# Seven products instead of eight for the first batch's Z, with the factors summed by accumulating transfers

## The chip, the cores and the metric

The kernel runs on one core of a Trainium2 chip. The metric is device time in microseconds for one execution. The kernel before was run three times: median 541.52 us (541.51 to 541.65). One execution more was profiled; the durations below are from that one.

## The reference

Four batches of 1024 tokens with 512 channels pass through one block of attention and a linear layer, each modulated by channels that come from a small conditioning vector:

```
mod = (silu(c) @ wmod), six vectors per batch: sa, ca, ga, sb, cb, gb
ga, gb = sign * max(|.|, 0.25)
h = layernorm(x) * (1 + ca) + sa
A = softmax over j of (h Wq^T)(h Wk^T)^T      (the same scores for all 16 heads)
x = x + ga * ((A (h Wv^T)) Wo^T)
h = layernorm(x) * (1 + cb) + sb
x = x + gb * (h @ (sum of 8 factors) / sqrt(8) + bias)
```

All is float32. The eight factors are 512 x 512 each; since their outputs are added, the kernel adds the factors first and multiplies once.

## The kernel before, in words

All heads have the same attention matrix, so per batch the kernel forms Z = N^T P^T, where N is the normalised input (1024 x 512) and P the exponentials of the scores (1024 x 1024, not yet divided by their sums). The output is then Z times one 512 x 512 matrix w (`make_w`, L696), which holds Wv, Wo, 1 + ca and ga. The reciprocal sums are multiplied in as a tile of output is added to x (L725); the shift sa becomes a row c1 that is added to every token (`add_c1`, L408).

Work is in tiles of 128 tokens, eight to a batch, in two groups ("halves") of four. Per batch, in the order in which the program is written:

- `ln1` (L395): statistics on VectorE, a power on POOL (L351), normalisation on VectorE (L365). Then the transposed copy: by TensorE for batch 0 (L378), for later batches by 32 x 32 transposes on VectorE (L437) and 16 DMAs that move blocks (`move_blocks`, L416 to L426, on SP's queue unless others are given).
- `scale_wqk` (L450): four multiplications on VectorE of the projection's weights by 1 + ca. `project` (L458): queries and keys of one half.
- `scores` (L505) for a pair of tiles: eight matmul records, a maximum on VectorE (L531), exponentials on ScalarE (L535). `transpose_probs` (L540) turns them by VectorE (L544) and 16 block moves; the first two pairs of batch 0 go through TensorE (`transpose_probs_pe`, L550), copied from PSUM by ScalarE (L561).
- Z in two halves of 512 columns. Batch 0 uses `z_steps` (L572): for each of four row blocks eight accumulated matmuls of 128 x 128 by 512 columns, and a copy by ScalarE (L592). In the trace each float32 matmul is two records, 128 in all. Batches 1 to 3 use `z_steps_by_seven` (L636): N and P are cut into quarters, and Z's four quarters come from seven products of sums of quarters (Strassen's method in the form with 15 additions). The sums of N are on POOL (`n_sums`, L612, lines L620 to L623, once a batch), those of P on VectorE (`p_sums`, L630, L633 and L634; L662 and L667 during the products), the sums of products on VectorE from PSUM (L672, L674, L677, L682, L688), two on POOL (L678, L679) and two copies on ScalarE (L660, L665). Each product is 16 records with 256 columns.
- `attn_out` (L716): four matmuls per tile of output, an addition to x on VectorE, statistics for the second layernorm.
- `ln2` (L734): as ln1, transposed by VectorE and block moves, scaled on ScalarE (L765). `make_f` (L705) multiplies the factor sum by gb on VectorE (L713); `ffn` (L771) is the last product, and its result goes out by DMA. `ffn` of one batch runs among the products of the next batch's Z.

What sets the order: each engine has its own queue, worked in order, and waits for semaphores in it. The steps have priorities that follow the text of the program, and a planner orders each engine's queue when the kernel is built, by its own estimate of when inputs are ready; `tc.keep_in_program_order` pins an instruction behind whatever was written before it on its engine. DMAs are issued from SP, ScalarE (ACT) and POOL; a DMA whose inputs are not ready holds up that engine's queue.

The parts around the change:

- The main loop for b = 0 (L821 to L841): Z's first half, the last softmax pair, `ln1` and the transposed copy of batch 1, `shift_rows` (c1 from its PSUM rows), `gates` (the two gates with `publish`, which stores rows to DRAM, L308), the eight c1 additions (L837), `second_channels`, `sum_factors`.
- `sum_factors` (L325): 16 loads of 512 KB on POOL's queue into four staging tiles of the pool `stg`, and 28 additions on POOL (L337, L340). A copy of one element by ScalarE (L331) keeps the first four from starting before Z's third row block is done.
- `spread` (L239) loads one row from DRAM to all 128 partitions, into two tiles with the tag "bc".
- Z's second half (L865 on): between its steps come batch 1's two projections and three softmax pairs (`places`), `make_w` after step 1; behind it `n_sums` of the next batch and `attn_out`, `ln2`, `p_sums` of the next batch.
- PSUM: four buffers of 512 columns (`psum_mm`) and two of 1024 for scores.

Of the kernel before, what the change touches and what calls it, by code (L numbers as in the profile page):

```python
# [30 lines left out]
def kernel(  # L31
# [19 lines left out]
    P = 128  # L51
# [273 lines left out]
    def sum_factors():  # L325
        for kc in range(KC):
            for r in range(0, NR, 2):
                f = stage(f"factor_{kc}_{r}").rearrange("p (r d) -> p r d", r=2)
                if kc == 0:

                    nc.scalar.copy(f[0:1, 0, 0:1], ZT[0, 0][0:1, 2, 0:1])  # L331
                nc.gpsimd.dma_start(
                    out=f, in_=factors[r : r + 2, ts(kc, P), :].rearrange("r p d -> p r d")
                )
                acc = fsum[:, kc, :]
                if r == 0:
                    nc.gpsimd.tensor_tensor(acc, f[:, 0], f[:, 1], ALU.add)  # L337
                else:
                    for k in range(2):
                        nc.gpsimd.tensor_tensor(acc, acc, f[:, k], ALU.add)  # L340
# [65 lines left out]
    bc_c1 = {}  # L406
# [21 lines left out]
    def hT_by_dma(b, g):  # L428
# [9 lines left out]
        move_blocks(st, hT.rearrange("p r k w -> p r (k w)"))  # L438
        return hT
# [100 lines left out]
    def transpose_probs(b, p):  # L540

        half, pair = divmod(p, 2)
        pr2 = probs[b, p][0]
        nc.vector.transpose(pr2, pr2)  # L544
        move_blocks(
            pr2.rearrange("p (c n) -> p c n", c=NQ),
            pt_tile(b, half)[:, pair].rearrange("p r j w -> p r (j w)"),
        )
# [17 lines left out]
    def softmax(b, p):  # L566
        scores(b, p)
        transpose_probs(b, p)

    ZT = {}  # L570

    def z_steps(b, half):  # L572

        zt = ztp.tile([P, KC, GW], F32, tag="zt", name=f"zt_{b}_{half}")
        ZT[b, half] = zt
        hold, steps = {}, []

        def part(dc, jh):
            if jh == 0:
                hold[dc] = psum_mm(f"ps_z_{b}_{half}_{dc}")  # L580
            for j in halves(jh):
                nc.tensor.matmul(  # L582
                    hold[dc], xn1[b, jh][:, j - jh * GT, ts(dc, P)], PT[b, half][:, :, :, j, :],
                    start=(j == 0), stop=(j == NT - 1),
                )
            if jh == 1:
                dst, src = zt[:, dc, :], hold[dc]
                if by_dma(b, half):

                    dst = dst.rearrange("p (h t r a) -> p h r t a", h=2, t=2, r=NQ)  # L590
                    src = src.rearrange("p (h r t a) -> p h r t a", h=2, t=2, r=NQ)
                nc.scalar.copy(dst, src)  # L592

        for dc in range(KC):
            for jh in range(2):
                steps.append(lambda dc=dc, jh=jh: part(dc, jh))
        return steps
# [38 lines left out]
    def z_steps_by_seven(b, half):  # L636
# [8 lines left out]
        def product(k, a, m):  # L645
            ps = psum_mm(f"ps_z_{b}_{half}_m{k}")
            for dc in range(2):
                for j in range(GT):

                    nc.tensor.matmul(  # L650
                        ps[:, ts(dc, 2 * P)], a[:, j, ts(dc, P)],
                        m[:, :, j].rearrange("p r (k a) -> p k r a", k=2),
                        start=(j == 0), stop=(j == GT - 1),
                    )
            return ps.rearrange("p (d i) -> p d i", d=2)
# [40 lines left out]
    def make_w(b):  # L696
        bc = spread("ga", b)
# [102 lines left out]
    for step in hT0[1][1]:  # L800
        step()
    first_channels(part)
# [10 lines left out]
    for jp in range(NT // 2):  # L813
        transpose_probs_pe(0, 1, jp)
    mod_rows(ps_mod_b, 4, rows_b)
# [3 lines left out]
    for b in range(B):  # L819
        nb = b + 1 if b + 1 < B else None  # L820
        if b == 0:  # L821
            z0 = z_steps(b, 0)
            z0[0]()
            softmax(0, 3)
            ln1(1, 0)
            hTn = [hT_by_dma(1, 0)]
            shift_rows(ps_c1)
            for step in z0[1:3]:
                step()
            ln1(1, 1)  # L830
            hTn.append(hT_by_dma(1, 1))
            gates()
            scale_wqk(nb)
            for step in z0[3:5]:
                step()

            add_c1(0, range(NT))  # L837
            for step in z0[5:]:
                step()
            second_channels()  # L840
            sum_factors()  # L841
        else:
            z0 = z_steps_by_seven(b, 0)
# [29 lines left out]
        for k, step in enumerate(z1):  # L873
# [3 lines left out]
            if b > 0 and k >= 3 and (nb is not None or k < 5):  # L877
# [62 lines left out]
```

## Time and profile before

| what | number |
|---|---|
| median of three runs | 541.52 us |
| the profiled execution, its own time | 538.85 us |
| its span, first to last instruction | 537.0 us |
| first record of Z, batch 0 | 56.84 us |
| first product of batch 1 (seven products) | 161.29 us |
| first product of batch 2 | 281.16 us |
| mean granted clock of TensorE | 0.996 |
| factor loads, first issue to last POOL addition | 80.95 to 145.6 us |

How to read it: the page has the busy time of each engine, the span in 40 slices, groups of equal instructions with mean durations, the chain of work that ended last, and DMA issues with the time to landing. The trace also answers for any stretch of the span. PE is TensorE, PEld its weight loads, DVE VectorE, ACT ScalarE, POOL GpSimd, SP the sync engine. Records of matmuls overlap: the sum of their durations is more than the time from the first to the last.

### The profile page before, as it was taken

Reading aid. Unit: us, or ns where it says so; the run is one execution under the profiler, and the core shown is the slowest. Engines: PE = TensorE matmul, PEld = TensorE weight load, DVE = VectorE, ACT = ScalarE, POOL = GpSimd, SP = SyncE. Lnnn points to the kernel's source line nnn. Section 1 sums busy time; section 2 is a strip of 40 time slices with the busy share of each in tenths; the row PEclk is TensorE's granted clock in tenths of the full one; section 3 lists DMA queues with packets and bytes.
Section 4 is the critical chain, followed back from the end, with each engine's and each line's share of the span. In section 5 each row is a group of like instructions: output and inputs, shape, how many; then the busy total and the mean of one; then the engine's idle time right before and its main releaser. Section 6 shows DMA issues by size and latency. Waiting matters only on the chain.

```text
span 537.0 us, 5254 instructions
## 1 busy us (share of the span) xinstructions
PE 523.4 (97%) x1688; PEld 290.9 (54%) x1688; DVE 362.1 (67%) x580; ACT 93.2 (17%) x155; POOL 158.5 (30%) x177
## 2 busy tenths in 40 slices
PE   6999899999999999999999999999999999999997
PEld 3533344433448457766448457765448457855444
DVE  4629987264899974359999965358999315577761
ACT  1327500122302020123102010123202200000110
POOL 1002136999801353323001343323001134021010
PEclk9989999999999999999999999999999999999999
DMA  8942369858444667404444656404444415001142
GB/s 319 380 182 68 89 179 262 247 165 244 109 118 113 174 209 226 134 1 97 118 113 113 183 157 209 110 0 99 122 119 107 142 59 214 21 0 32 47 157 78
DMA packets 39570, 74.07 MB, mean 138 GB/s; under 512 B 9988, under 2 KB 10756, under 8 KB 39544
## 3 DMA queue, kind: packets, MB, share of 16 engines
q1 hardware_dynamic: 27368, 41.06, 26.8%
q0 software_dynamic: 8624, 28.48, 17.0%
q10 hardware_dynamic: 3552, 4.21, 2.9%
q8 instruction: 13, 0.21, 0.2%
q14 instruction: 13, 0.11, 0.1%
HBM read 35.93 MB, written 8.42 MB: 83 GB/s over the span
## 4 chain that ended last, share of the span: by engine, by line
PE 58%; DVE 20%; issue 8%; SPq 5%; DMA 4%; POOL 3%; ACT 2%; DVEq 0%; POOLq 0%; ACTq 0%
PE ps_z_m L650 17%; PE ps_f L779 15%; PE ps_z L582 8%; PE ps_qk L469 5%; PE ps_o L720 5%; SPq L426 5%; PE ps_wvo L186 3%; DVE pr L544 3%; DVE nm L531 2%; DMA pt<-pr 2%; PE ps_sc L515 2%; ACT pr L535 2%; DVE hT_f L365 2%; DVE x L725 1%; DVE bn_a L356 1%
## 5 line engine op out<-in xcount | busy, mean ns | idle before, releaser
L779 PE MATMUL ps_f<-f,hT_f 128*128 128x512 f32 (+1 forms) x264 | 111.8, 580 | 0.8 <-ACT hT_f L765 0.5
L720 PE MATMUL ps_o<-w,zt 128*128 128x512 f32 x256 | 111.8, 594 | 0.5 <-DVE zt L688 0.5
L779 PEld LDWEIGHTS ps_f<-f,hT_f 128*128 128x128 f32 x264 | 49.9, 190 | 59.4 <-issue 54.3
L720 PEld LDWEIGHTS ps_o<-w,zt 128*128 128x128 f32 x256 | 48.3, 190 | 61.2 <-issue 56.4
L650 PE MATMUL ps_z_m<-pt,xn_a 128*128 128x256 f32 x288 | 65.3, 380 | 0.0
L650 PEld LDWEIGHTS ps_z_m<-pt,xn_a 128*128 128x128 f32 x288 | 54.6, 190 | 11.4 <-issue 2.4
L582 PE MATMUL ps_z<-pt,xn_a 128*128 128x512 f32 x128 | 56.9, 597 | 0.0
L784 DVE TENSOR_TENSOR x<-ps_f,x 128x512 f32<-128x512 f32 (+1 forms) x33 | 21.9, 670 | 43.8 <-PE ps_f L779 43.8
L535 ACT ACTIVATE pr<-ps_sc,nm 128x1024 f32<-128x1024 f32 x32 | 35.5, 1111 | 79.1 <-DVE nm L531 40.9
L650 PE MATMUL ps_z_m<-pt,s 128*128 128x256 f32 x192 | 43.6, 380 | 0.0
L650 PEld LDWEIGHTS ps_z_m<-pt,s 128*128 128x128 f32 x192 | 36.3, 190 | 8.5 <-issue 3.9
L582 PEld LDWEIGHTS ps_z<-pt,xn_a 128*128 128x128 f32 x128 | 23.8, 190 | 31.6 <-issue 30.8
L515 PE MATMUL ps_sc<-kT,qT 64*128 64x512 f32 x128 | 38.2, 626 | 2.3 <-ACT pr L535 2.3
L531 DVE TENSOR_REDUCE nm<-ps_sc 128x1 f32<-128x1024 f32 x32 | 37.6, 1210 | 2.4 <-PE ps_sc L515 2.4
L765 ACT ACTIVATE hT_f<-st_f,mod_sb,mod_cb 128x512 f32<-128x512 f32 x28 | 20.6, 803 | 96.6 <-DVE bn_f L356 40.2
L351 POOL TENSOR_TENSOR r_f<-v_f,mhalf 128x4 f32<-128x4 f32 x8 | 9.3, 1165 | 94.8 <-DVE v_f L347 94.8
L725 DVE SCALAR_TENSOR_TENSOR x<-ps_o,ri,x 128x512 f32<-128x512 f32 x32 | 23.8, 743 | 15.1 <-PE ps_o L720 15.0
L544 DVE STREAM_TRANSPOSE pr<-pr 128x2048 f32<-128x2048 f32 x14 | 32.2, 2299 | 0.9 <-DMA pt<-pr 0.7
L351 POOL TENSOR_TENSOR r_a<-v_a,mhalf 128x4 f32<-128x4 f32 x8 | 9.2, 1152 | 78.8 <-DVE v_a L347 78.6
L340 POOL TENSOR_TENSOR fsum<-fsum,factor 128x512 f32<-128x512 f32 x24 | 30.4, 1273 | 0.4
L469 PE MATMUL ps_qk<-hT_a,wqk 128*128 128x512 f32 x64 | 30.5, 624 | 0.0
L483 DVE TENSOR_SCALAR qT<-ps_qk,qbias 64x512 f32<-64x512 f32 x8 | 5.9, 743 | 36.1 <-PE ps_qk L469 36.1
(124 smaller groups left out, 582.7 us busy)
## 6 DMA issues: line engine op xcount, KB each, us to landing
pt<-pr SPq DMA_DIRECT2D x224, 64.0 KB, 2.0
factor<-in_factors_dram POOLq DMA_DIRECT2D x16, 512.0 KB, 5.1
hT_a<-st_a SPq DMA_DIRECT2D x96, 64.0 KB, 4.9
out_dram<-x POOLq DMA_DIRECT2D x24, 256.0 KB, 2.6
x<-in_x_dram POOLq DMA_DIRECT2D x24, 256.0 KB, 5.3
xa<-in_x_dram POOLq DMA_DIRECT2D x20, 256.0 KB, 4.0
st_f<-hT_f SPq DMA_DIRECT2D x62, 64.0 KB, 2.0
st_f<-hT_f ACTq DMA_DIRECT2D x60, 64.0 KB, 2.1
```

Source lines behind the costliest of these rows:

```text
L340: nc.gpsimd.tensor_tensor(acc, acc, f[:, k], ALU.add)
L426: queues[i % len(queues)].dma_start(out=dst[ts(c, Q), r], in_=src[ts(r, Q), c])
L469: nc.tensor.matmul(ps[: 2 * R, :], wqkb[b][:, kc, :], hT[:, kc] if b == 0 else hT[:, :, kc], start=(kc == 0), stop=(kc == KC - 1),)
L515: nc.tensor.matmul(ps[:, ts(h, 512)], qT[h * R : (h + 1) * R, ts(i, P)], kT[h * R : (h + 1) * R, :], start=True, stop=True,)
L531: nc.vector.tensor_reduce(nm, ps, AX.X, ALU.max, negate=True)
L535: nc.scalar.activation(pr, ps, AF.Exp, bias=nm, scale=1.0, accum_out=den[:, k : k + 1])
L544: nc.vector.transpose(pr2, pr2)
L582: nc.tensor.matmul(hold[dc], xn1[b, jh][:, j - jh * GT, ts(dc, P)], PT[b, half][:, :, :, j, :], start=(j == 0), stop=(j == NT - 1),)
L650: nc.tensor.matmul(ps[:, ts(dc, 2 * P)], a[:, j, ts(dc, P)], m[:, :, j].rearrange("p r (k a) -> p k r a", k=2), start=(j == 0), stop=(j == ...
L720: nc.tensor.matmul(ps, ZT[b, half][:, kc, ts(j, P)], wb[b][:, kc, :], start=(kc == 0), stop=(kc == KC - 1),)
L725: nc.vector.scalar_tensor_tensor(xi, ps, rinv[b][:, t : t + 1], xi, ALU.mult, ALU.add)
L779: nc.tensor.matmul(ps, hT2[b, g][:, kc, ts(j, P)], fb[b][:, kc, cols], start=(kc == 0), stop=(kc == KC - 1),)
```

## The change

Batch 0's Z is made by the seven products as well; the old `z_steps` is deleted and `z_steps_by_seven` takes its name. With it come `n_sums(0)` in the start, behind the transposes of batch 0's input, and `p_sums(0, 0)`, `p_sums(0, 1)`. For the first half, whose P was transposed by TensorE, the order of columns needs no rearrangement (`by_dma`).

The staging tiles now hold batch 0's sums of N, and the factors go straight to their sum: 32 transfers of 256 KB on POOL's queue in eight rounds of four, of which the first round writes and the other seven add to what is there. Each is pinned behind what was written before it on POOL. Round 0 comes at the end of batch 0's first half, rounds 1 to 3 after steps 1, 3 and 5 of the second half, 4 and 5 among the first output tiles, 6 and 7 among the later ones.

The block moves of the last softmax pair of batch 0 and of batch 1's second transposed copy alternate between SP's and ACT's queues. `shift_rows` and `gates` move, ga's and c1's rows are spread ahead of the second half, and the c1 additions come two at a time in the last four steps of the second half, as in the other batches. The second projection weights' first place is after step 1 instead of step 0.

```diff
-    def sum_factors():
-        for kc in range(KC):
-            for r in range(0, NR, 2):
...
-                nc.gpsimd.dma_start(
-                    out=f, in_=factors[r : r + 2, ts(kc, P), :].rearrange("r p d -> p r d")
-                )
...
+    def add_factor(r):
+        for kc in range(KC):
+            kw = {} if r == 0 else {"accum_op": ALU.add}
+            tc.keep_in_program_order(
+                nc.gpsimd.dma_start(out=fsum[:, kc, :], in_=factors[r, ts(kc, P), :], **kw)
+            )
...
-    def z_steps_by_seven(b, half):
+    def z_steps(b, half):
...
+                    q = m[:, :, j]
+                    if by_dma(b, half):
+                        q = q.rearrange("p r (k a) -> p k r a", k=2)
                     nc.tensor.matmul(
-                        ps[:, ts(dc, 2 * P)], a[:, j, ts(dc, P)],
-                        m[:, :, j].rearrange("p r (k a) -> p k r a", k=2),
+                        ps[:, ts(dc, 2 * P)], a[:, j, ts(dc, P)], q,
...
-        bc = spread("ga", b)
+        bc = bc_ga[b] if b in bc_ga else spread("ga", b)
...
     for step in hT0[1][1]:
         step()
+    n_sums(0)
     first_channels(part)
...
         transpose_probs_pe(0, 1, jp)
+    p_sums(0, 0)
     mod_rows(ps_mod_b, 4, rows_b)
...
         if b == 0:
+            both = nc.sync, nc.scalar
             z0 = z_steps(b, 0)
             z0[0]()
-            softmax(0, 3)
+            softmax(0, 3, *both)
+            z0[1]()
+            shift_rows(ps_c1)
+            z0[2]()
             ln1(1, 0)
             hTn = [hT_by_dma(1, 0)]
-            shift_rows(ps_c1)
-            for step in z0[1:3]:
+            for step in z0[3:5]:
                 step()
             ln1(1, 1)
-            hTn.append(hT_by_dma(1, 1))
-            gates()
-            scale_wqk(nb)
-            for step in z0[3:5]:
-                step()
-
-            add_c1(0, range(NT))
+            hTn.append(hT_by_dma(1, 1, *both))
             for step in z0[5:]:
                 step()
+            scale_wqk(nb)
+            gates()
             second_channels()
-            sum_factors()
+
+            bc_ga[0], bc_c1[0] = spread("ga", 0), spread("c1", 0)
+            add_factor(0)
...
-            p_sums(b, 1)
-        z1 = z_steps(b, 1) if b == 0 else z_steps_by_seven(b, 1)
+        p_sums(b, 1)
+        z1 = z_steps(b, 1)
...
-            places = (0, 2, 3, 4, 5)
+            places = (1 if b == 0 else 0, 2, 3, 4, 5)
...
-            if b > 0 and k >= 3 and (nb is not None or k < 5):
+            if b == 0 and k in (1, 3, 5):
+                add_factor((k + 1) // 2)
+            if k >= 3 and (nb is not None or k < 5):
...
                 if t == 2:
                     scores(nb, 3)
+                if b == 0 and t % 2:
+                    add_factor((t + 7) // 2)
             ln2(b, 0)
...
             p_sums(nb, 0)
+            if b == 0:
+                add_factor(6)
         for t in halves(1)[2:]:
             attn_out(b, t)
+        if b == 0:
+            add_factor(7)
         ln2(b, 1)
```

More of the change, by code (lines that the diff above doesn't have):

```diff
@@ L323, in stage @@
         return stg.tile([P, 1024], F32, tag="stg", name=name)
-    def sum_factors():
+    def add_factor(r):
         for kc in range(KC):
-            for r in range(0, NR, 2):
-                f = stage(f"factor_{kc}_{r}").rearrange("p (r d) -> p r d", r=2)
-                if kc == 0:
-                    nc.scalar.copy(f[0:1, 0, 0:1], ZT[0, 0][0:1, 2, 0:1])
-                nc.gpsimd.dma_start(
-                    out=f, in_=factors[r : r + 2, ts(kc, P), :].rearrange("r p d -> p r d")
-                )
[L335 to L340, printed above, removed]
+            kw = {} if r == 0 else {"accum_op": ALU.add}
+            tc.keep_in_program_order(
+                nc.gpsimd.dma_start(out=fsum[:, kc, :], in_=factors[r, ts(kc, P), :], **kw)
+            )
     def rstd_of(mv, tiles, name):
@@ L404, in ln1 @@
             load_xa(b + g, 1 - g)
-    bc_c1 = {}
+    bc_c1, bc_ga = {}, {}
     def add_c1(b, tiles):
@@ L426, in move_blocks, with hT_by_dma @@
             queues[i % len(queues)].dma_start(out=dst[ts(c, Q), r], in_=src[ts(r, Q), c])
-    def hT_by_dma(b, g):
+    def hT_by_dma(b, g, *queues):
         st = stp.tile([P, NQ, KC * GT * Q], F32, tag="st", name=f"st_a_{b}_{g}")
@@ L437, in hT_by_dma @@
             nc.vector.transpose(blocks[:, t], xn1[b, g][:, t, :])
-        move_blocks(st, hT.rearrange("p r k w -> p r (k w)"))
+        move_blocks(st, hT.rearrange("p r k w -> p r (k w)"), *queues)
         return hT
@@ L538, in scores, with transpose_probs @@
         nc.vector.reciprocal(rinv[b][:, 2 * p : 2 * p + 2], den)
-    def transpose_probs(b, p):
+    def transpose_probs(b, p, *queues):
         half, pair = divmod(p, 2)
@@ L546, in transpose_probs @@
             pr2.rearrange("p (c n) -> p c n", c=NQ),
-            pt_tile(b, half)[:, pair].rearrange("p r j w -> p r (j w)"),
+            pt_tile(b, half)[:, pair].rearrange("p r j w -> p r (j w)"), *queues,
         )
@@ L564, in transpose_probs_pe, with softmax @@
         )
-    def softmax(b, p):
+    def softmax(b, p, *queues):
         scores(b, p)
-        transpose_probs(b, p)
+        transpose_probs(b, p, *queues)
     ZT = {}
[L572 to L597, printed above, removed]
     CW = D // 2
@@ L821 @@
         if b == 0:
+            both = nc.sync, nc.scalar
             z0 = z_steps(b, 0)
             z0[0]()
-            softmax(0, 3)
+            softmax(0, 3, *both)
+            z0[1]()
+            shift_rows(ps_c1)
+            z0[2]()
             ln1(1, 0)
             hTn = [hT_by_dma(1, 0)]
-            shift_rows(ps_c1)
-            for step in z0[1:3]:
+            for step in z0[3:5]:
                 step()
             ln1(1, 1)
-            hTn.append(hT_by_dma(1, 1))
-            gates()
-            scale_wqk(nb)
-            for step in z0[3:5]:
-                step()
-            add_c1(0, range(NT))
+            hTn.append(hT_by_dma(1, 1, *both))
             for step in z0[5:]:
                 step()
+            scale_wqk(nb)
+            gates()
             second_channels()
-            sum_factors()
+            bc_ga[0], bc_c1[0] = spread("ga", 0), spread("c1", 0)
+            add_factor(0)
         else:
-            z0 = z_steps_by_seven(b, 0)
+            z0 = z_steps(b, 0)
             for k, step in enumerate(z0):
```

## The prediction

> **What bounds the kernel now.** I read the page's busy row first, then the slices, the groups of matmuls, the chain of waits, and last the busy time by stretches of batch 0 and batch 1.
>
> ```profile
> span 537.0 us, 5254 instructions
> ...
> PE 523.4 (97%) x1688; PEld 290.9 (54%) x1688; DVE 362.1 (67%) x580; ACT 93.2 (17%) x155; POOL 158.5 (30%) x177
> ```
>
> TensorE is busy in 97% of the span; the slices show it short of 9 tenths only in the first, the fifth and the last one. So time goes away when TensorE gets less to do, provided that what feeds it keeps pace. The groups show the two forms of Z, and the chain of waits shows what sixteen records of each take end to end:
>
> ```profile
> L650 PE MATMUL ps_z_m<-pt,xn_a 128*128 128x256 f32 x288 | 65.3, 380 | 0.0
> ...
> L582 PE MATMUL ps_z<-pt,xn_a 128*128 128x512 f32 x128 | 56.9, 597 | 0.0
> ```
>
> ```profile
> 97.76 6.87 PE ps_z L582 x16
> ...
> 189.40 3.45 PE ps_z_m L650 x16
> ```
>
> Matmuls overlap, so I use the 6.87 and 3.45 us per sixteen, not the 597 and 380 ns of one. The stretches set batch 0's first half of Z (56.8 to 87.2), its second half up to batch 1's first product (87.2 to 161.3), and the same second stretch of batch 1, which has the seven products already (213.3 to 281.2). Columns after the two times: length, busy us (count) of PE, PEld, DVE, ACT, POOL, then clock, DMA share, GB/s.
>
> ```profile
> core 0: us, PE busy (x) PEld busy (x) DVE busy (x) ACT busy (x) POOL busy (x), PEclk, DMA share, GB/s
> 56.80:87.20 30.40, 30.40 (x80) 13.25 (x79) 23.87 (x40) 5.98 (x14) 9.13 (x14) 1.00 0.59 161
> 87.20:161.30 74.10, 72.94 (x178) 30.28 (x178) 48.61 (x60) 14.33 (x25) 55.83 (x48) 1.00 0.69 188
> ...
> 213.30:281.20 67.90, 67.34 (x226) 38.86 (x226) 50.42 (x69) 13.13 (x22) 14.51 (x8) 1.00 0.37 96
> ```
>
> **TensorE's own gain.** Batch 0's Z is 128 records of 512 columns: 8 x 6.87 = 54.96 us. After the change it is 2 halves x 7 products x 16 records of 256 columns: 14 x 3.45 = 48.30. That is 6.66 us less, 3.33 in each half. The first half: 30.40 - 3.33 = 27.07.
>
> For the second half batch 1 is a measurement of nearly the new program: the same seven products, two projections, four softmaxes, eight output tiles and the sums for the next batch. It takes 67.90 where batch 0 takes 74.10, 6.20 less. 3.33 of this are the products. Of the rest, about 0.6 is a shorter wait for the exponentials (1.17 against 0.56) and 1.91 is one score group: at 104.56 and 112.67 batch 0 runs its first scores as two groups of four records, 1.91 each, because the second half of the transposed input came late; batch 1 runs eight in 1.92. The change sends half of those block moves over ACT's queue (SP's now run without a break from 55.40 to 100.65, 64 moves), so I take all 6.20. Sum so far: -3.33 - 6.20 = **-9.53**.
>
> **n_sums(0) on POOL meets VectorE at the start.** The trace has no work on POOL from 17.6 to 47.6. The four sums need only the normalised tiles, ready at 20.74, so they run from about 20.8: 4 x 2.35 (the rows at L620 to L623) end at 30.2. In this time VectorE scales the weights of the first projection, which TensorE waits for. What such a meeting costs is seen when batch 1's scaling met the factor sums:
>
> ```profile
> 26.17 0.29 DVE L453 TENSOR_SCALAR wqk<-wqk,mod_ch_a 128x128 f32<-128x128 f32 x1
> ...
> 27.36 0.67 DVE L453 TENSOR_SCALAR wqk<-wqk,mod_ch_a 128x128 f32<-128x128 f32 x3
> ```
>
> ```profile
> 111.06 1.35 DVE L453 TENSOR_SCALAR wqk<-wqk,mod_ch_a 128x128 f32<-128x128 f32 x1
> 111.08 1.26 POOL L337 TENSOR_TENSOR fsum<-factor 128x512 f32<-128x512 f32 x1 [0.99 <-DMA factor<-in_factors_dram]
> ```
>
> An instruction of 0.28 became 1.35: it ended with POOL's 1.26. So the scaling at 26.17 ends with the third sum at about 27.9, and the next one with the fourth at 30.3 instead of 27.6. TensorE wants that second chunk two matmuls after 27.11, at 0.55 each (the granted clock was 0.81 there), so at 28.2. Cost 30.4 - 28.2 = **+2.2**, passed on whole, since scores, exponentials and transposes follow one another down to Z at 56.84. Bounds: 0, if the scaling goes first; 4 x 2.35 - 0.67 = 8.7, if each scaling waits for one sum.
>
> **VectorE.** Added in batch 0: four sums of P (4 x 1.22), two each of L662 and L667 (4 x 1.2), ten additions from PSUM (10 x 0.69): 16.6 us. Gone: the factor sums on POOL (28 x 1.27) no longer block it. The w products show what that is worth:
>
> ```profile
> 88.97 7.33 DVE L700 SCALAR_TENSOR_TENSOR w<-wvo,mod_ch_a,bc_ga 128x512 f32<-128x512 f32 x4
> ...
> 207.23 2.73 DVE L700 SCALAR_TENSOR_TENSOR w<-wvo,mod_ch_a,bc_ga 128x512 f32<-128x512 f32 x4
> ```
>
> That is 4.6, and 2.97 - 0.86 = 2.1 for the scaling at 110.87: net +9.9. The two stretches held 72.5 us of VectorE in 104.5; they would hold 82.4 in 95. The first half alone is over-full: 23.87 + 2.4 + 2.4 + 3.45, less the 3.2 us of c1 adds in it that move to the second half, is 28.9 in 27.1 us. TensorE needs of it only t for the second product (L633, ready about 1 us before TensorE gets there, as scores fill in), the sum of L662, and emptied PSUM buffers, of which there are four. The gates (some 6 us of small rows between 64.8 and 78.8) now stand behind this work and can be late: w is first wanted when batch 0's output tiles start, near 120. I cost this at 0; cover gone, see rival 2. The four zt adds on POOL (1.27 each) lie beside the next product, as in batch 1. ACT loses four copies and gets 16 block moves at 0.64, 10 us in stretches where it is busy 6 of 30.
>
> **The factors.** 16 transfers of 512 KB and 28 additions become 32 transfers of 256 KB, 28 of them accumulating, at 0.56 of POOL each (the 256 KB rows at L243). Each waits on POOL for the one before it on the same quarter, and the zt adds, the variances' powers and the load of the FFN gate stand behind it in POOL's queue. Rounds 0 to 3 lie some 7 to 12 us apart. The tight ones are 6 and 7: round 6 is pinned behind POOL's power of ln2, round 7 follows it, and VectorE's f products read the sum. Batch 1's rows give the distances:
>
> ```profile
> 273.46 1.03 POOL L351 TENSOR_TENSOR r_f<-v_f,mhalf 128x4 f32<-128x4 f32 x1 [13.19 <-DVE v_f L347]
> ...
> 281.16 3.62 PE L650 MATMUL ps_z_m<-pt,xn_a 128*128 128x256 f32 x16
> ...
> 283.64 0.69 DVE L713 TENSOR_TENSOR f<-fsum,bc_gb 128x512 f32<-128x512 f32 x1
> ```
>
> The first quarter of round 6 leaves 9.1 us before the first f product. If a transfer lands l after its issue, round 7's first quarter lands 2 l later, so VectorE stands for 2 l - 9.1, and the work behind it (ln2's second half, L662, the next batch's ln1) is just in time for TensorE: the chain of waits runs through it from 265 to 302. The trace has no accumulating transfer. Plain ones:
>
> ```profile
> factor<-in_factors_dram POOLq DMA_DIRECT2D x16, 512.0 KB, 5.1
> ...
> out_dram<-x POOLq DMA_DIRECT2D x24, 256.0 KB, 2.6
> x<-in_x_dram POOLq DMA_DIRECT2D x24, 256.0 KB, 5.3
> ```
>
> Lower bound 2.6 (stall 0); upper bound twice the load's 5.3, as it also reads its destination: 10.6 (stall 12.1). The nearest row is the load of 256 KB from HBM, 5.3: 2 x 5.3 - 9.1 = **+1.5**, which I take.
>
> The Trainium skill, "DMA: Bandwidth & Descriptors", section "Anatomy of one DMA — SWDGE (gpsimd) path", puts a transfer at a fixed 2 us plus its bytes over 436 GB/s: 2.6 us for 256 KB as an estimate, no stall, and a sum lower by 1.5; the loads in this trace took twice that, so I do not use it.
>
> **Sum.** -9.53 + 2.2 + 1.5 = -5.8 us. The profiled execution took 538.85 (span 537.0 and 1.85 around it), so it would be 533.0; the shown runs have a median of 541.52, 2.67 above, and from there I predict **535.7**.
>
> **Rivals.**
> 1. *The accumulating rounds are late (slower).* One mechanism: round 7 behind round 6 in front of the f products. It eats -9.53 + 2.2 = -7.3 from 2 l - 9.1 = 7.3, l = 8.2 us on. At l = 10.6: -7.3 + 12.1 = +4.8, 546.3. For it: a second read and a wait per round; the DMA share was 0.94 in 80 to 100. Against: few other bytes move then (0.37 of the engines in batch 1's stretch).
> 2. *VectorE is the bound in the first half.* If it works its 28.9 us in an order that holds up the second product or the PSUM buffers, most of that half's 3.33 is lost: about 539.0. For it: no slack left; against: 6.7 us of blocking gone, and free time in the second half.
> 3. *No meeting at the start and fast rounds:* -9.53, 532.0. For it: only 4 short scalings are at stake.
> 4. *The second half does not become batch 1's:* if the inputs stay late, it gains 3.33 instead of 6.20: 538.6, inside the forecast's spread.
>
> **Chances.** Forecast (531.5 to 539.5) with rival 4: 0.52; rival 1: 0.20; rival 2: 0.18; rival 3: 0.10. About 0.2% (1.1 us) is what a measurement of this kernel can tell from no change. Rival 1 is slower in 0.16, within 0.2% in 0.03, faster in 0.01; rival 2 is slower in 0.03 and the same in 0.04, where its loss is near double. Faster 0.74, same 0.07, slower 0.19. The range 531.0 to 545.0 leaves out rival 3's best and rival 1's worst.
>
> **What would show it.** L582 gone and 896 records at L650 (672 now and 224). The first projection ending near 38 instead of 35.9, with L453 of 1 to 2 us at 26 to 30: the start. First product of batch 1 near 154 instead of 161.3 (-9.53 + 2.2), 1.1 of it gone by the end of the first half. L700 at 2.7. L713 of batch 0 with an idle time before it released by the accumulating DMA: 1 to 2 us in the forecast, over 8 in rival 1. After batch 1's first product all distances as before (119.87 from batch to batch). The prediction is wrong if TensorE has gaps over 2 us between 57 and 154, or if the distance from batch 1's to batch 2's first product grows.

## The result and the profile after

The changed kernel takes **550.33 us** (median of five runs, 550.22 to 551.6), the kernel before, run beside it, 541.51. The ratio is 1.0174 (95% interval 1.0159 to 1.019): 1.7% slower, where 535.7 us and a gain were predicted, and above the upper end of the range, 545.0. The profiled execution took 550.23 us, 548.3 of it span; that of the kernel before took 538.85 and 537.0. So the traces differ by 11.3 us. The medians differ by less, 8.8, because the profiled execution of the kernel before lay 2.67 under its median and that of the changed kernel 0.10 under its own.

The page, its first lines and the slices of TensorE and its granted clock:

```profile
span 548.3 us, 5454 instructions
...
PE 519.4 (95%) x1784; PEld 310.6 (57%) x1784; DVE 378.2 (69%) x598; ACT 90.3 (16%) x147; POOL 153.1 (28%) x173
...
PE   6999898999992799999999999999999999999997
...
PEclk9979999999997799999999999999999999999999
```

TensorE has 4 us less to do than before (523.4) in a span 11.3 us longer. The hole is in the 13th and 14th slice, 164 to 192 us, and the clock is down to 7 tenths in it. By stretches (columns as in the prediction): first half of Z, second half up to batch 1's first product, and the 23.5 us after that.

```profile
60.20:88.80 28.60, 27.15 (x128) 22.36 (x127) 27.25 (x39) 4.19 (x8) 7.55 (x9) 1.00 0.60 152
88.80:157.90 69.10, 67.97 (x225) 38.76 (x226) 51.32 (x68) 13.17 (x22) 35.17 (x37) 1.00 0.77 164
157.90:168.40 10.50, 10.50 (x49) 8.82 (x47) 9.26 (x15) 0.00 (x0) 6.13 (x7) 1.00 0.90 162
168.40:181.40 13.00, 0.00 (x1) 0.00 (x0) 6.53 (x13) 0.00 (x0) 2.76 (x4) 0.65 0.88 206
```

The two halves of Z are close to the forecast: 28.6 and 69.1 us, where 27.07 and 67.9 were predicted and 30.4 and 74.1 taken before. Up to batch 1's first product the kernel is ahead, 157.88 against 161.29. Then comes a stretch of 13 us in which TensorE does nothing. The timeline of TensorE names what ended it:

```profile
157.88 3.62 PE L618 MATMUL ps_z_m<-pt,xn_a 128*128 128x256 f32 x16
...
181.43 5.89 PE L618 MATMUL ps_z_m<-pt,s 128*128 128x256 f32 x16 [13.03 <-DVE pt L629]
```

It waits for VectorE's second sum of P of batch 1 (L629, L662 before). The 16 records behind the wait take 5.89 us instead of 3.62, at a granted clock of 0.62. VectorE is late for two reasons. The first is in its own timeline, at the products of the factor sum and gb (L680, L713 before):

```profile
172.40 0.69 DVE L680 TENSOR_TENSOR f<-fsum,bc_gb 128x512 f32<-128x512 f32 x1 [4.63 <-DMA fsum<-in_factors_dram]
174.69 0.69 DVE L680 TENSOR_TENSOR f<-fsum,bc_gb 128x512 f32<-128x512 f32 x1 [0.99 <-DMA fsum<-in_factors_dram]
```

With the other two, VectorE stands 7.1 us for rounds 6 and 7. POOL's timeline shows them, first issue of round 6 and of round 7:

```profile
158.45 3.89 POOL L331 DMA_DIRECT2D fsum<-in_factors_dram  x4
163.40 0.85 POOL L331 DMA_DIRECT2D fsum<-in_factors_dram  x1 [1.06 <-DMA fsum<-in_factors_dram]
```

The second reason is that VectorE reached these products already late. The block moves that transpose batch 1's probabilities are 64 DMAs on SP's queue, and SP issues one when the queue takes it (start, length of the run of issues). First the kernel before, then the changed one:

```profile
120.21 42.09 SPq L426 DMA_DIRECT2D pt<-pr  x64
```

```profile
118.08 59.81 SPq L418 DMA_DIRECT2D pt<-pr  x64
```

They start 2 us earlier and end 15.6 us later, at 177.9. Rounds 3 to 5 are issued from 122.5 to 140, rounds 6 and 7 from 158.5, among them. The moves are slow in just these stretches: here the moves beside rounds 3 to 5, then those between round 5 and round 6 (count, ns of one issue as min/median/max, first and last start; below it the time to landing).

```profile
L418 SPq DMA_DIRECT2D pt<-pr x22: 588/816/2129, 122.4 to 145.6; - x22
DMA to landing us min/median/max: 2.0/5.3/6.8
```

```profile
L418 SPq DMA_DIRECT2D pt<-pr x18: 525/588/592, 146.9 to 157.6; - x18
DMA to landing us min/median/max: 1.9/2.0/2.0
```

From 158.3 on the median to landing is 5.2 us again. By the DMA share, the last number but one of a line (the profile's count, which can pass 1), the DMA engines are full in these two stretches and less than half busy between them:

```profile
122.50:145.00 22.50, 22.45 (x66) 10.43 (x63) 16.83 (x19) 3.08 (x6) 13.39 (x15) 1.00 1.02 197
158.50:172.00 13.50, 9.90 (x46) 8.28 (x45) 9.26 (x15) 0.00 (x0) 7.27 (x8) 1.00 0.97 183
147.00:158.00 11.00, 11.00 (x27) 4.87 (x26) 9.97 (x14) 2.30 (x4) 0.55 (x1) 1.00 0.44 108
```

ScalarE's exponentials, which overwrite what the moves read, wait for the moves:

```profile
137.20 1.11 ACT L527 ACTIVATE pr<-ps_sc,nm 128x1024 f32<-128x1024 f32 x1 [13.92 <-DMA pt<-pr]
...
149.86 1.11 ACT L527 ACTIVATE pr<-ps_sc,nm 128x1024 f32<-128x1024 f32 x1 [10.36 <-DMA pt<-pr]
```

Before, the longest of these waits were 7.97 and 2.33 us:

```profile
134.82 1.11 ACT L535 ACTIVATE pr<-ps_sc,nm 128x1024 f32<-128x1024 f32 x1 [2.33 <-DMA pt<-pr]
...
145.10 1.11 ACT L535 ACTIVATE pr<-ps_sc,nm 128x1024 f32<-128x1024 f32 x1 [7.97 <-DMA pt<-pr]
```

From batch 2's first product on (292.81, 281.16 before) the two kernels keep the same distances, to 0.4 us at the end of the span. So the loss has three places: the start, where Z begins 3.37 us later (60.21), Z itself, where 6.8 us are gained, and the distance from batch 1's to batch 2's first product, which is 134.93 us instead of 119.87: **15.06 us lost**. 3.37 - 6.8 + 15.06 = 11.6, the 11.65 by which batch 2 begins later.

### The profile page after: what moved, and what is told of

It reads as the page before. It is cut to its first block, busy times and chain, and to the rows that moved or that the text cites. A ratio compares the mean times of both kernels' runs of the same rounds, so it can differ in the third digit from the quotient of the medians.

```text
span 548.3 us, 5454 instructions
## 1 busy us (share of the span) xinstructions
PE 519.4 (95%) x1784; PEld 310.6 (57%) x1784; DVE 378.2 (69%) x598; ACT 90.3 (16%) x147; POOL 153.1 (28%) x173
## 4 chain that ended last, share of the span: by engine, by line
PE 45%; issue 16%; DVE 15%; SPq 9%; DMA 6%; POOL 5%; ACT 1%; ACTq 1%; POOLq 0%; DVEq 0%
PE ps_z_m L618 19%; PE ps_f L746 16%; SPq L418 9%; PE ps_o L687 5%; PE ps_qk L461 4%; DMA fsum<-in_factors_dram 3%; DVE pr L536 2%; DVE hT_f L357 1%; ACT pr L527 1%; DVE bn_a L348 1%; DVE nm L523 1%; POOL r_a L343 1%; ACTq L418 1%; DVE xn_a L357 1%; DMA st_f<-hT_f 1%
## 5 line engine op out<-in xcount | busy, mean ns | idle before, releaser
L618 PE MATMUL ps_z_m<-pt,xn_a 128*128 128x256 f32 x384 | 87.3, 380 | 1.5 <-DVE zt L649 1.5
L618 PEld LDWEIGHTS ps_z_m<-pt,xn_a 128*128 128x128 f32 x384 | 72.5, 190 | 17.3 <-issue 2.6
L618 PE MATMUL ps_z_m<-pt,s 128*128 128x256 f32 x256 | 60.5, 391 | 13.0 <-DVE pt L629 13.0
L618 PEld LDWEIGHTS ps_z_m<-pt,s 128*128 128x128 f32 x256 | 49.8, 196 | 25.3 <-DVE pt L629 13.4
L507 PE MATMUL ps_sc<-kT,qT 64*128 64x512 f32 x128 | 36.4, 626 | 1.6 <-ACT pr L527 1.6
L627 ACT COPY zt<-ps_z_m 128x512 f32<-128x512 f32 x8 | 4.7, 585 | 183.3 <-PE ps_z_m L618 106.9
L331 POOL DMA_DIRECT2D fsum<-in_factors_dram x32 | 28.0, 1014 | 18.6 <-DMA fsum<-in_factors_dram 18.2
L618 PE MATMUL ps_z_m<-t,s 128*128 128x256 f32 x128 | 29.1, 380 | 0.6 <-DVE t L598 0.6
L754 POOL DMA_DIRECT2D out_dram<-x x24 | 13.2, 549 | 58.5 <-DVE x L751 48.2
L618 PE MATMUL ps_z_m<-t,xn_a 128*128 128x256 f32 x128 | 29.2, 381 | 0.0
```

Source lines behind the costliest of these rows:

```text
L331: nc.gpsimd.dma_start(out=fsum[:, kc, :], in_=factors[r, ts(kc, P), :], **kw)
L507: nc.tensor.matmul(ps[:, ts(h, 512)], qT[h * R : (h + 1) * R, ts(i, P)], kT[h * R : (h + 1) * R, :], start=True, stop=True,)
L618: nc.tensor.matmul(ps[:, ts(dc, 2 * P)], a[:, j, ts(dc, P)], q, start=(j == 0), stop=(j == GT - 1),)
```

## The experiments

The theory: the rounds cost twice, once as a wait ahead of the products with gb and once by slowing the block moves. Rivals: one of the two alone; the order of POOL's queue; the seven products themselves. "Distance" below is the time from batch 1's to batch 2's first product, "moves" the length of SP's 64 moves, "f wait" VectorE's wait for the factor sum, all from the traces; times are medians. A trace is of one execution, whose own time can lie off the median: 540.88 us with rounds 0, 6 and 7, 549.53 with the rounds in the gaps, 552.92 for the kernel before with accumulating rounds.

| kernel | time, us | ratio to before (95%) | batch 1's first product | distance | moves | f wait |
|---|---|---|---|---|---|---|
| before | 541.5 | | 161.29 | 119.87 | 42.09 | 0 |
| changed | 550.33 | 1.0174 (1.0159 to 1.019) | 157.88 | 134.93 | 59.81 | 7.1 |
| plain writes | 543.64 | 1.0046 (1.0026 to 1.0067) | 162.26 | 124.57 | 48.51 | 3.6 |
| one round | 535.19 | 0.9888 (0.9872 to 0.9904) | 158.34 | 119.87 | 40.41 | 0 |
| rounds 6, 7 earlier | 552.41 | 1.0211 (1.0167 to 1.0255) | 165.59 | 128.62 | 57.85 | 0 |
| all rounds early | 560.12 | 1.0352 (1.033 to 1.0373) | 184.18 | 119.87 | 40.45 | 0 |
| rounds 0, 6, 7 | 543.62 | 1.0045 (1.0029 to 1.0061) | 157.66 | 125.82 | 46.29 | 5.9 |
| rounds 0 to 5 | 545.14 | 1.0074 (1.0051 to 1.0096) | 160.26 | 127.87 | 51.49 | 0 |
| rounds in gaps | 546.88 | 1.0101 (1.0064 to 1.0139) | 172.25 | 119.87 | 40.52 | 0 |
| in gaps, sums held | 541.76 | 1.0041 (1.0009 to 1.0072) | 164.46 | 119.86 | 40.53 | 0 |
| **rounds spread** | **532.45** | **0.9851 (0.9819 to 0.9883)** | 155.44 | 119.87 | 40.42 | 0 |
| before, accumulating | 550.89 | 1.0189 (1.0148 to 1.023) | 168.43 | 126.51 | 47.72 | 6.4 |
| changed, sums held | 548.77 | 1.013 (1.0083 to 1.0177) | | | | |
| one round, sums held | 532.73 | 0.9852 (0.9826 to 0.9878) | 155.12 | 119.85 | 40.45 | 0 |

**Plain writes.** The same transfers at the same places, without the addition:

```diff
-            kw = {} if r == 0 else {"accum_op": ALU.add}
+            kw = {}
```

> The changed kernel with all eight rounds of factor transfers as plain writes (the adding is left out, so the factor sum holds the last factor alone); pins, waits and bytes from HBM stay. Theory 1, the adding itself is what is slow (a round 4 to 10 us, and it holds up the block moves that share the DMA engines): 535 to 538 us, the 64 block moves of batch 1's probabilities back to about 42 us, no wait before batch 0's f products over 2 us. Theory 2, the pin behind ln2's power and the waits in a row are the cause, whatever the transfer does: over 545. Theory 3, the factors are not the cause, VectorE is over-full: about 550.

The same bytes cost less when they do not accumulate. An issue on POOL takes 0.54 us instead of 0.86, and the median to landing is shorter; here that of plain writes, then that of the changed kernel:

```profile
fsum<-in_factors_dram POOLq DMA_DIRECT2D x32, 256.0 KB, 4.8
```

```profile
fsum<-in_factors_dram POOLq DMA_DIRECT2D x32, 256.0 KB, 6.4
```

The moves take 48.51 us, 8.1 above the 40.41 without seven of the rounds; the other 11.3 of the changed kernel's 19.4 come with the addition. So traffic on POOL's queue slows the moves, and accumulating traffic slows them more. None of the three theories has its time, though: theory 1 wanted 535 to 538 us, moves of 42 and no wait over 2 us, and the plain writes are still 8.5 us above the kernel with one round. 4.7 of these are distance; 3.9 lie ahead of batch 1's first product, where the faster rounds let POOL's sums of N for batch 1 meet VectorE's scaling of the projection's weights, which takes 5.70 us instead of 0.86.

**One round.**

```diff
-        for kc in range(KC):
+        for kc in range(KC if r == 0 else 0):
```

> The changed kernel with only the first of the eight rounds (the other seven factors are left out). Theories 1 and 2: the rest of the change alone, 533 to 537 us: 541.5 less 9.5 in TensorE's stretches, plus 3.4 at the start and 1.5 in the first half. Theory 3: about 550.

```profile
118.89 40.41 SPq L418 DMA_DIRECT2D pt<-pr  x64
```

No wait for factors, moves back to 40.41, and the distance exactly that of before: 535.19. The seven rounds cost 15.1 us, and all else in the change is a gain, ratio 0.9888. That the products cause the loss is out.

**Rounds 6 and 7 earlier.** They are written right behind round 5, so that they no longer stand behind ln2's power on POOL:

```diff
                 if b == 0 and t % 2:
-                    add_factor((t + 7) // 2)
+                    for r in (4,) if t == 1 else (5, 6, 7):
+                        add_factor(r)
...
-            if b == 0:
-                add_factor(6)
...
-        if b == 0:
-            add_factor(7)
```

> The changed kernel with rounds 6 and 7 written right behind round 5, ahead of ln2's first half, so that they are no longer pinned behind its power. Theory 1: the wait before the f products goes (7.1 us of VectorE), the slow block moves stay: 542 to 546. Theory 2: 535 to 538. Theory 3: about 550.

The wait for the factors is gone, and the time is not better: 552.41, near the time of theory 3, which the run with one round has excluded. VectorE now waits for the moves in front of the first sum of P:

```profile
157.09 1.23 DVE L598 TENSOR_TENSOR t<-pt 128x1024 f32<-128x1024 f32 x1 [7.21 <-DMA pt<-pr]
```

"Only the wait before f" falls with this: taken away, it comes back as a wait for transposed probabilities. The new wait lies ahead of batch 1's first product, which is 7.7 us later than in the changed kernel (165.59 against 157.88), while the distance is 6.3 us shorter.

**All rounds early**, from 30.6 us on, pinned among the sums and the first softmax pairs:

```diff
     n_sums(0)
+    for r in range(3):
+        add_factor(r)
...
+    add_factor(3)
...
+    add_factor(4)
```

and so on, one behind each step of the start.

> The changed kernel with the rounds moved to the time in which the DMA engines have nothing to do: 0 to 2 behind n_sums(0), the others one by one up to the second product of batch 0's first half (about 30 to 85 us). Theories 1 and 2: no wait before the f products and block moves of batch 1's probabilities at about 42 us: 534 to 538, a little above the run with one round if the rounds hold up the block moves of the first half. Theory 3: about 550.

A miss: 560.12. The moves after 100 us and the distance are those of before, but POOL works in order. Its power for batch 1's layernorm stands behind the rounds until 76.53 (50.93 in the changed kernel), and VectorE waits for it:

```profile
77.94 0.55 DVE L357 TENSOR_SCALAR xn_a<-xa,mv,r_a 128x512 f32<-128x512 f32 x1 [22.79 <-POOL r_a L343]
```

The first issues of the rounds follow each other by some 6 us (30.6, 36.3, 40.7, 47.4). This run also shows what fills these 6 us. From 59 to 76 us the accumulating transfers are the only ones that are issued, and the DMA engines are full with them alone, a share of 1.04 at 175 GB/s; first the stretch, then its only line of DMA issues:

```profile
59.00:76.00 17.00, 1.71 (x6) 0.71 (x6) 0.00 (x0) 0.00 (x0) 9.65 (x12) 0.63 1.04 175
```

```profile
fsum<-in_factors_dram POOLq DMA_DIRECT2D x12, 256.0 KB, 5.9
```

At that rate the 1.05 MB of a round take 6.0 us. The plain loads at the start of the changed kernel (4 to 24 us) fill the engines as much, 1.05, and move 377 GB/s. So the rounds leave little room for other transfers while they run; what the engines do with the time inside an accumulating transfer, no trace here shows. Eight rounds in a row kept POOL's queue for 46 us (30.57 to 76.53).

**The two losses apart.** Rounds 1 to 5 left out, and rounds 6 and 7 left out:

```diff
-        for kc in range(KC):
+        for kc in range(KC if r in (0, 6, 7) else 0):
```

> Leaves out factors 1 to 5 (rounds 1 to 5 issue nothing), so the factor sum is of three factors only. The changed kernel is 15.1 us above the kernel with one round; this run is to give one share of it. Theory (two separate losses): rounds 6 and 7 still land late, so the multiplications by gb wait some 3 to 7 us for them, but batch 1's 64 block moves run beside few factor bytes and go back to 40 to 43 us: 538 to 542 us. Rival (one loss, the block moves alone): the wait is hidden by other work and the time is that of one round, 535 to 536 us. Second rival (one loss, the wait alone): the whole 15 us stay, 548 to 551 us.

```diff
-        for kc in range(KC):
+        for kc in range(KC if r < 6 else 0):
```

> Leaves out factors 6 and 7 (rounds 6 and 7 issue nothing). Theory (two separate losses): no wait ahead of the multiplications by gb, but the 64 block moves still take 52 to 60 us beside rounds 1 to 5, and VectorE gets its transposed probabilities late: 542 to 547 us. Rival (the block moves alone): all of the loss stays, 548 to 551 us. Second rival (the wait alone): 535 to 536 us, as with one round.

TensorE's waits at the same place, first with rounds 0, 6 and 7, then with rounds 0 to 5:

```profile
172.81 5.18 PE L618 MATMUL ps_z_m<-pt,s 128*128 128x256 f32 x16 [4.62 <-DVE pt L629]
```

```profile
176.98 5.66 PE L618 MATMUL ps_z_m<-pt,s 128*128 128x256 f32 x16 [6.21 <-DVE pt L629]
```

Each part alone lengthens the distance, by 5.95 and 8.00 us; together that is 13.95 of the 15.06. The first median lies above its forecast (543.62 for 538 to 542), the second inside (545.14 for 542 to 547). Two losses, then, that come one behind the other before VectorE's one sum. How nearly they add is less sure than the traces look: by the medians the two runs are 8.4 and 10.0 us above the kernel with one round, 18.4 together, where the changed kernel is 15.1 above it, and the trace with rounds 0, 6 and 7 is of the fastest of ten executions. Which loss is which does show. With rounds 0, 6 and 7 VectorE stands 5.9 us for the factors, as much as the distance grows; the moves that are longer there (46.29 in all) are the last of the 64, which serve the second half, and no later wait of TensorE for them is seen. With rounds 0 to 5 nothing waits for the factors, and the slow moves are those of the first two softmax pairs, which this sum of P needs. The f waits of the first of the two runs (total, count, longest):

```profile
DVE f L680 <- DMA fsum<-in_factors_dram: 5.9, 4, 3.3
```

**Rounds in the gaps** of SP's queue: 0 to 2 behind the sums of N, 3 to 5 behind batch 1's loads, 6 and 7 behind the spread of c1's row:

```diff
     n_sums(0)
+    for r in range(3):
+        add_factor(r)
...
             hTn = [hT_by_dma(1, 0)]
+            for r in range(3, 6):
+                add_factor(r)
...
-            add_factor(0)
+            add_factor(6)
+            add_factor(7)
```

> All eight rounds, computed in full, put where SP's queue moves few blocks: rounds 0 to 2 behind the sums of N in the start (about 30 to 52 us), 3 to 5 behind the loads of batch 1's first half (about 55 to 72), 6 and 7 behind the spread of c1's row (about 92 to 106). Theory (the loss is in the place of the transfers: beside batch 1's block moves, and late for the multiplications by gb): both losses go, block moves after 100 us at 40 to 45 us for 64, 535 to 538 us, which is faster than the kernel before. Rival (accumulating transfers cost the same wherever they run, since POOL's queue waits in order for each round and other bytes are moved in these stretches too): ln1's power on POOL or the moves before 100 us become late, 545 us or more.

546.88, with executions from 543.55 to 549.94: by the median the rival's case. Both losses behind 100 us are gone, but the gap is none: the 24 moves of the last softmax pair of batch 0 take 26.66 us instead of 16.44, the moves of batch 1's transposed input end 13.9 us later behind them (110.70 against 96.83), and TensorE waits for that input:

```profile
108.41 6.54 PE L461 MATMUL ps_qk<-hT_a,wqk 128*128 128x512 f32 x8 [10.33 <-DMA hT_a<-st_a]
```

**The same with the sums of N held** until the first projection's weights are scaled:

```diff
-    n_sums(0)
...
     scale_wqk(0)
+    n_sums(0)
...
+        if b == 0:
+            nc.scalar.copy(s1[0:1, 0, 0:1], wqkb[0][0:1, KC - 1, 0:1])
```

> As the run with rounds in the gaps, and the four sums of N on POOL are held by one copied element on ScalarE until VectorE has scaled the first projection's weights. Theory (of the 3.4 us by which Z starts later than in the kernel before, 2.5 come from VectorE's scaling beside POOL's sums: 1.13 and 2.75 us a tile where 0.29 and 0.67 are usual): the four multiplications are back at 0.3 to 0.7 us, Z's first record is 2 to 3 us earlier than with the rounds in the gaps alone, and so is the end, unless POOL's sums are then late for the first product that reads them. Rival (the start is late from the input's arrival or from something else): Z's start and the end move by less than 0.7 us.

541.76, by the medians 5 us better than without the hold; the executions spread from 540.94 to 549.42, and the two intervals overlap. The scaling is back at 0.28 and 0.67, and batch 0's third pair of scores begins at 42.06 us instead of 46.27. Rounds 0 to 2 now start 8 us later, though, and POOL's power for batch 1 comes behind them:

```profile
54.53 1.46 DVE L357 TENSOR_SCALAR xn_a<-xa,mv,r_a 128x512 f32<-128x512 f32 x3 [7.49 <-POOL r_a L343]
```

TensorE waits 7.76 us for transposed probabilities after that, so Z begins at 64.16 us, 3.55 later than without the hold, where the theory wanted it 2 to 3 earlier. The gain has another place: the moves of batch 1's transposed input end at 105.89 instead of 110.70, and TensorE waits 2.1 us for that input instead of 10.33. Two places are to be mended: this one, and rounds 3 to 5 beside the moves.

**Rounds spread.** Round 0 is held as the sums are; rounds 0 to 2 go between the sums, 3 and 4 behind batch 1's loads with the last sum between them, 5 to 7 behind the spread of c1's row:

```diff
+        if b == 0:
+            for held in (fsum[0:1, 0, 0:1], s1[0:1, 0, 0:1]):
+                nc.scalar.copy(held, wqkb[0][0:1, KC - 1, 0:1])
+            add_factor(0)
         tt(s1, a21, a22, ALU.add)
+        if b == 0:
+            add_factor(1)
         tt(a21, a11, a21, ALU.subtract)
         tt(s2, s1, a11, ALU.subtract)
-        tt(s4, a12, s2, ALU.subtract)
+        if b == 0:
+            add_factor(2)
+            last_sum.append(lambda: tc.keep_in_program_order(tt(s4, a12, s2, ALU.subtract)))
...
             hTn = [hT_by_dma(1, 0)]
+            add_factor(3)
+            last_sum[0]()
+            add_factor(4)
...
-            add_factor(0)
+            for r in range(5, 8):
+                add_factor(r)
```

> All eight rounds, computed in full, at places chosen from the two runs with rounds in the gaps: the start of round 0 and of the sums of N is held until the first projection's weights are scaled, rounds 0 to 2 go between these sums (about 30 to 47 us, to be over before batch 1's power on POOL, which was 7.5 us late for VectorE in the last run), 3 and 4 behind batch 1's loads (51 to 63), 5 to 7 behind the spread of c1's row (88 to 108). Theory (the part costs only where its rounds hold up a queue that is waited for): no wait of TensorE for batch 0's transposed probabilities, at most 1 us for batch 1's transposed input, 64 block moves in 40 to 43 us, and the time is that of one round (535.2) less some 4 us of the start: 530 to 533 us. Rival (eight rounds of about 6 us on POOL's queue have no 48 us to spare wherever they go): another wait of 4 to 10 us comes up in the first 130 us, 538 to 544 us.

532.45 us, ratio 0.9851 (0.9819 to 0.9883): faster than both kernels and as forecast (530 to 533). The page, then POOL's timeline with round 2, the power for batch 1 and the last issue of round 7, then SP's moves:

```profile
span 530.7 us, 5461 instructions
...
PE 516.2 (97%) x1784; PEld 309.5 (58%) x1784; DVE 372.4 (70%) x598; ACT 90.7 (17%) x149; POOL 153.8 (29%) x173
```

```profile
43.34 4.66 POOL L331 DMA_DIRECT2D fsum<-in_factors_dram  x4
47.24 1.82 POOL L343 TENSOR_TENSOR r_a<-v_a,mhalf 128x4 f32<-128x4 f32 x1
...
106.73 0.86 POOL L331 DMA_DIRECT2D fsum<-in_factors_dram  x1 [0.62 <-DMA fsum<-in_factors_dram]
```

```profile
115.99 40.42 SPq L418 DMA_DIRECT2D pt<-pr  x64
```

Round 2's issues are over at 48.0, about when batch 1's power is wanted, round 7's at 107.6, 8 us ahead of the moves, and no line has a wait of TensorE over 2.3 us after the start.

**The kernel before with the accumulating rounds alone.** Z and all else as before:

```diff
-            sum_factors()
+            add_factor(0)
...
+            if b == 0 and k in (1, 3, 5):
+                add_factor((k + 1) // 2)
```

and rounds 4 to 7 at the changed kernel's places.

> The kernel before, with one part of the change alone: the factors are summed by accumulating transfers in eight rounds at the places where the changed kernel has them; Z of batch 0, the sums and all else stay. Theory (the part by itself turns the change into a loss, because the rounds slow batch 1's block moves and end late for the multiplications by gb): the 64 block moves go from 42 us to 55 to 60, the multiplications by gb wait 4 to 8 us, and the time is 547 to 556 us. Rival (the rounds do harm only in the changed kernel, whose second half is shorter and whose sums keep VectorE busy): 540 to 544 us.

550.89, ratio 1.0189: this one part makes the old kernel as slow as the whole change does. The mechanism is only half the one expected. The moves take 47.72 us, not 55 to 60: here rounds 0 to 5 are over at 121 and the moves begin at 127.33, so only rounds 6 and 7 fall on them, and rounds 0, 6 and 7 made 46.29 above. The wait for the factors is there,

```profile
174.45 0.69 DVE L705 TENSOR_TENSOR f<-fsum,bc_gb 128x512 f32<-128x512 f32 x1 [3.39 <-DMA fsum<-in_factors_dram]
```

and 6.64 us are lost in the distance. Batch 1's first product is 7.14 us later as well: here the spread of ga's row stands behind the rounds on POOL, and the w products wait 7.46 us for it. In the changed kernel that row is spread ahead of the rounds.

**The hold alone**, in the changed kernel and in the kernel with one round; the diff is that of the sums held.

> The changed kernel with one edit: the four sums of N on POOL are held by a copied element on ScalarE until VectorE has scaled the first projection's weights; the rounds stay where the change put them. Theory (4 us of the start, the slow scaling and the lower clock behind TensorE's wait, are a loss of their own): the scaling is back at 0.3 to 0.7 us a tile, Z begins 3.5 to 4.5 us earlier, and the end too: 545.5 to 547.5 us. Rival (the gain is taken back behind it, since the rounds and block moves end when they end): Z begins earlier but the end moves by less than 1 us, 549.5 to 550.5 us.

Inconclusive: its runs spread from 545.85 to 555.53, and the interval, 1.0083 to 1.0177, reaches that of the changed kernel. The profiled execution is the longest of them, and nothing is read from it.

> The kernel with one round (seven factors left out), and the four sums of N on POOL held until VectorE has scaled the first projection's weights. It differs by that hold alone from the kernel with one round (535.2 us), where nothing of the factors is waited for. Theory (the start has a price of its own: the slow scaling, TensorE's wait and the lower clock behind it): the scores of batch 0 begin some 4 us earlier and the time is 530 to 532 us, at or below that of the kernel with the rounds spread (532.5), so that spreading the rounds costs at most 2 us. Rival (the gain of the last run came from somewhere else and the start's is taken back by VectorE in the first half): 534.5 to 535.5 us.

This run answers it better: 532.73 against 535.19 with one round, 0.7 above its forecast, intervals 0.9826 to 0.9878 and 0.9872 to 0.9904, which overlap by 0.0006. Z begins at 56.94 us instead of 61.01; 1.16 of these 4.07 us are there before the hold can act (17.92 against 19.08 for the last of the first weight products, L186). So the start has a price of its own, 1.9 us by the ratios, 2.5 by the medians, 3.3 by the spans. And seven rounds more, well placed, cost nothing that these runs can tell: 532.45 with all eight, ratio 0.9851 against 0.9852.

## Why the prediction was wrong

By the traces, up to batch 2's first product (predicted -5.8, measured +11.65):

| term | predicted, us | measured, us | from |
|---|---|---|---|
| Z's first half | -3.33 | -1.8 | 88.79 - 60.21 against 87.19 - 56.84 |
| second half | -6.20 | -5.0 | 157.88 - 88.79 against 161.29 - 87.19 |
| sums of N at the start | +2.2 | +3.37 | 60.21 against 56.84 |
| rounds | +1.5 | +15.06 | 134.93 against 119.87 |

- **The failed step is the factors**, +1.5 us in the sum and +15.06 measured. The prediction costed the rounds by one thing, the distance of round 7 to the f products, and named that as rival 1. It gave the rival the sign that came, and 546.3 us at most. The landing time was too short: round 6 is first issued at 158.45, round 7 at 163.40, and the first f product starts at 172.40, so the two landings take 4.95 and 9.00 us, 13.95 together and 7.0 in the mean, not 5.3. The wait that follows is 4.63 us at the first of the four products and 7.1 over all four. But with 13.95 rival 1's own sum is -7.3 + (13.95 - 9.1) = -2.5, still a gain; it turns into a loss only from l = 8.2 us on. So rival 1 had the sign by luck: its wait alone does not make the loss.
- **What was left out weighs more.** "Against: few other bytes move then" was read from batch 1's stretch, at a DMA share of 0.37, and taken as a reason why the rounds would be quick. The other direction was never priced: what the rounds do to the 64 small moves that share the DMA engines. Those went from 40.41 to 59.81 us, and rounds 0 to 5 alone, which nothing waits for, cost 8.00 us of distance through them. Accumulating transfers fill the DMA engines by themselves (1.04 above), so together with the 0.37 of batch 1's stretch they ask for more than there is. The rounds ahead of 6 were passed over ("Rounds 0 to 3 lie some 7 to 12 us apart"; they began at 92.46, 98.72, 103.18 and 122.46), though 3 to 5 fall on the moves. The paragraph on VectorE counts ACT's 16 block moves at 0.64 us each, as if an issue on a DMA queue had one duration; SP's took 0.51 to 2.13. The trace of before gave little warning: with its plain factor loads about, the same 64 moves took 42.09.
- The Trainium skill, "Trainium Kernel Development and Optimization", section "Key Constraints", says that DMAs issued from the SP, ACT and POOL queues run on the same 16 DMA engines and interleave. The runs agree: transfers on POOL's queue lengthen moves on SP's, from 40.41 to 59.81 us.
- **The start** was right in mechanism and nearly in size. The scaling took 1.13 for one and 2.75 for three instead of 0.29 and 0.67, as here:

```profile
26.93 1.13 DVE L445 TENSOR_SCALAR wqk<-wqk,mod_ch_a 128x128 f32<-128x128 f32 x1
...
28.12 2.75 DVE L445 TENSOR_SCALAR wqk<-wqk,mod_ch_a 128x128 f32<-128x128 f32 x3
```

  TensorE waited 0.20 and 0.90 us for it. Another 0.76 us are lost ahead of anything that the change touches: the first weight products (L186) begin 0.30 us later, when their load has landed, and take 0.47 longer. That leaves 2.6 of the 3.37 for the change. What the waits do not account for, 1.5 us, goes with the clock that the prediction did not price: 0.61 and 0.54 from 28 to 36 us, where the kernel before had 0.62 and then 1.00.
- **The first half** gained half of what was forecast. TensorE stood 1.45 us for a PSUM buffer that VectorE had not emptied (L649), which is rival 2 in small: VectorE was busy 27.25 of 28.60 us.
- **The second half** became batch 1's, as predicted, within 1.2 us (69.1 for 67.9); 0.59 us of that is a wait for the first sum of P. L667 is back at 2.07 and 0.75 us. The moved gates, the powers on POOL and the zt adds cost nothing that shows.
- **The base.** The prediction added 2.67 us, the distance of the profiled execution from the median of the kernel before. That distance did not carry over: it is 0.10 in the changed kernel. So 2.6 us of the error of the terms, 17.5 in all, were given back, 0.3 at the end of the span, and 14.6 remain between 535.7 and 550.33. Why the kernel before has executions at 538 and at 541.5 us is open; no trace here shows the slower kind.

## What to carry to other kernels

Price a DMA that you add in both directions: how late it lands for its reader, and what it does to every transfer on the same engines while it runs, small moves on another queue above all. How full it makes the engines by itself is the number to look for. Accumulating transfers take the additions off an engine and give back a chain of rounds in POOL's queue, each waiting for the last; find them places where nothing on POOL is waited for and no other queue moves blocks, and check each place by the next reader, for a wait taken away in one place came up in the next four times here. When a change loses, take its parts alone: with seven of the eight rounds taken out, the rest of this one was 1.1% faster than the kernel before.

## What the runs showed of the hardware that was not expected

- An accumulating transfer of 256 KB occupies POOL for 0.86 us (plain 0.54) and lands after 6.4 us in the median (plain 4.8 at the same places). Accumulating transfers alone kept the DMA engines full at 175 GB/s, where plain loads moved 377 GB/s; rounds of four, each waiting for the last, follow each other by about 6 us.
- 64 moves of 64 KB on SP's queue took 40.41 us alone, 48.51 beside plain writes on POOL's queue and 59.81 beside accumulating ones.
- TensorE's granted clock falls after a wait, and not always: the 16 records behind the 13.03 us took 5.89 us at 0.62, but after a wait of 1.45 us (one round, sums held) 16 records took 5.41 at 0.69, and after one of 1.45 in the changed kernel 3.72 at 1.00. The Trainium skill, "TensorE: Matmul & The Clock Gate", section "Why this matters for your kernels", asks for no idle gaps over about 3 us between bursts of matmuls; the long wait agrees; of the two short ones, which lie below it, one was followed by the low clock all the same.
